# A sparse attention layer: one unit joined on VectorE, part of the last batch weighed by GpSimd, and a written place for every operation

## The chip, the cores and the metric

The kernel runs on one core of one Trainium2 chip. A core has engines with queues of their own that run side by side and meet at semaphores: TensorE (PE in the profile, with its weight loads as PEld), VectorE (DVE), ScalarE (ACT), GpSimd (POOL) and SyncE (SP), which only issues DMA here. The metric is the device time of one execution in microseconds (us); smaller is better.

## The reference, cut to what matters

```python
# x: (16, 1024, 512), adj: (1024, 1024) of 0 and 1, with the diagonal set; W: (512, 512); H, HD = 8, 64
h = jnp.maximum(_layernorm(x, axis=-1), 0.0)
q, k, v = ((h @ W + b).reshape(16, 1024, H, HD) for W, b in ((Wq, bq), (Wk, bk), (Wv, bv)))
scores = jnp.einsum('bihd,bjhd->bhij', q, k) / jnp.sqrt(64.0)
scores = scores + jnp.where(adj == 0, -1e9, 0.0)
weights = jax.nn.softmax(scores, axis=-1)
return x + jnp.einsum('bhij,bjhd->bihd', weights, v).reshape(16, 1024, 512)
```

The adjacency is sparse and very uneven: a few rows have many neighbours, most have a handful. All data are 32-bit floats.

## The kernel before, in words

The kernel never forms the full score matrix. It ranks the 1024 nodes by degree once, cuts the ranked order into eight tiles of 128 rows (tile 0 has the longest rows, tile 7 the shortest), and gives each tile a fixed number of neighbour slots (`CAPS`: 11, 8, 6, 5, 4, 3, 3, 2). What is left of long rows of tile 0 is cut into pieces of four neighbours; the pieces of all rows fill one more group, called tile -1, whose results are added to their owners' rows with a matmul by an owner matrix (`owner_t`).

Slots are handled in *units* of two to four slots (`PARTS`, `UNITS`): fourteen units a batch, four of them for tile 0: (0,0), (-1,0), (0,4) and (0,8), where a pair is the tile and the first slot. In the program's numbering they are units 10 to 13.

For each of the 16 batches, and with two batches in flight at a time:

- `load_x` (GpSimd, an indirect load by the ranked order), `stats`, `variance`, `power`, `shift` and `norm` make the normalized rows; `flip` transposes them on TensorE and `unflip` copies them to SBUF (ScalarE).
- `proj_kv` makes keys and values on TensorE, `evict_kv` copies them out of PSUM, and `store_kv` writes them to a table in DRAM. All eight tiles of a batch must be stored before its first gather.
- `queries` projects the queries of a tile (TensorE). For the pieces, `copy_q` and a matmul by `owner` spread tile 0's queries to the pieces.
- `gather` (GpSimd, an indirect DMA of 512 KB for each slot; the row itself comes by a plain DMA from SP) brings key and value rows of the neighbours into one of six buffers `g`.
- `multiply` and `score` (VectorE) make the scores of a unit, `exponent` (ScalarE) the weights, `row_sums` (VectorE) their sums.
- The values are weighed slot by slot: `weigh_v` on VectorE, `weigh_s` on ScalarE, with eight activations, one for each head, for a slot.
- `fold` adds the slots of a unit to one (VectorE, some on GpSimd). In batches 0 to 14 tiles 1 to 7 are then summed over their units by `join` on VectorE; tile 0's four units are summed by `add_up` on TensorE, in PSUM. In the last batch nothing but tile 7 is folded, and every slot of the other tiles is added by `add_up`.
- `scale` divides by the row sum, `residual` adds x, and `put_out` scatters the 128 rows to the output by an indirect DMA of GpSimd.

The order of all this is not left to a compiler: `planned` lists every operation with its engine, what it follows and which buffers it uses, and in the kernel before a planner (`Plan.ordered`) runs that list against assumed lengths (`LENGTHS`) and priorities (`AT`, `FINE`), and so fixes the order of each engine's queue. The engines then run their queues in order, each waiting at semaphores where data or a buffer isn't ready. Buffers are counted in `POOLS`: 16 for x, 6 for g, 3 for kvt, 2 each for the PSUM tiles of keys and values, queries and sums, 1 for the scaled result `o`.

Where a unit of tile 0 is summed, in `add_up`:

```python
count = 1 if folds(b, B, t, count) else count
for s in range(count):
    nc.tensor.matmul(ACC[b, home], owner_t if t < 0 else ident, v[:, s, :], ...)
```

In the profile L1103 is `multiply`, L1107 `score`, L1111 `exponent`, L1123 `weigh_v`, L1129 `weigh_s`, L1134 `fold`, L1141 `join`, L1157 `add_up`, L1070 the matmul that spreads queries to the pieces, L843 and L841 the projections and their bias, L1093 the gathers, L1207 the sum with x and L1210 `put_out`.

Of the kernel before, what the change touches and what calls it, by code (L numbers as in the profile page):

```python
# [25 lines left out]
F32 = mybir.dt.float32  # L26
# [6 lines left out]
P = 128  # L33
H = 8
# [26 lines left out]
LAST_TILES = (0, 1, 2, 3, 4, 5, 6, 7)  # L61
LAST_ORDER = tuple(UNITS.index(unit) for t in LAST_TILES for unit in PARTS[t])
LAST_DIRECT = (7,)
POOL_FOLDS = ((5, 0), (4, 0), (1, 0), (1, 4), (-1, 0))
# [6 lines left out]
BY_VECTOR_LAST = {2: 1, 3: 1, 4: 1}  # L71
VECTOR_RESIDUAL = (4,)
AT = dict(
    load_x=170.09, stats=-5.83, variance=-6.1, power=-47.58, shift=-11.83, norm=-65.99, flip=-3.5, unflip=-69.44, proj_kv=-0.17,
    evict_kv=-1.04, queries=-0.21, own=7.45, gather=-8.51, score=1.54, exponent=37.66, row_sums=-33.29, share=-103.18,
    weigh_v=-4.42, weigh_s=56.4, fold=-4.42, join=-3.58, add_up=-5.47, direct_residual=3.86, direct_out=-0, more=-116.77,
    pass_on=-0.94, sums=-5.02, scale=-1.48, residual=-38.62, put_out=-47.81, seen=11.6, zero=-5.59, zero_rate=0.56,
    ahead=-14.69, early=0.02, early2=0.33, early3=0.24, first=-60.83, first_rate=7.61, v_late=9.54, key_row=-221.51,
    rank_row=-80.11, rank_d=-9.75, rank_a=45.47, ranks=-75.78, ends=-96.51, list_of=76.9, tell=-79.58, spread=-44.68,
    others=-101.81, spots=-59.47, long_rows=-152.98, long_0=-64.75, long=-72.37, longest=20.9, count=-6.64, pieces=2.43,  # L80
    setup=-64.27, parts=-10.1, spread_bias=-5.47, copy_q=131.7, fetch_q=-35.12, evict_v=0.78, bias_v=-48.9,
)
FINE = {
    ('owners',): -1.5, ('rank_of', 0): 5.46, (-1, 'evict_kv', 7, 0): 0.78, (-1, 'proj_kv', 2, 1): 6.9,
    (-1, 'proj_kv', 6, 0): 9.56, (-1, 'proj_kv', 7, 0): 8.02, (0, 'multiply', 4): 10.01, (0, 'queries', 0, 1): -1.48,
    (0, 'queries', 0, 7): 5, (0, 'weigh_s', 5, 0): -10.62, (1, 'evict_kv', 3, 1): -0.64, (1, 'flip', 1): 0.71,
    (1, 'fold', 11, 1, 1): 0.79, (1, 'fold', 12, 2, 2): 2.15, (1, 'fold', 8, 1, 1): 1.26, (1, 'fold', 8, 2, 2): 2.12,
    (1, 'gather', 8, 3): 0.98, (1, 'join', 9): 3.14, (1, 'multiply', 5): 1.61, (1, 'multiply', 6): 1.34,
    (1, 'proj_kv', 0, 0): -0.95, (1, 'proj_kv', 2, 0): 1.26, (1, 'put_out', 0, 4): -1.57, (1, 'put_out', 0, 5): -2.25,
    (1, 'score', 13): -5.29, (1, 'score', 5): 3.73, (1, 'score', 9): -0.38, (1, 'shift', 1): 3.92, (1, 'weigh_s', 6, 1): 1.85,  # L90
    (1, 'weigh_v', 11): -2.61, (1, 'weigh_v', 9): -1.9, (2, 'add_up', 1): 3.15, (2, 'add_up', 3): 6.42,
    (2, 'evict_kv', 5, 1): 3.83, (2, 'gather', 12, 0): 1.34, (2, 'gather', 3, 1): -1.6, (2, 'gather', 4, 2): -1.63,
    (2, 'gather', 6, 2): -2.75, (2, 'gather', 7, 2): -2.05, (2, 'gather', 8, 3): -1.07, (2, 'gather', 9, 0): 2.03,
    (2, 'gather', 9, 1): 2.13, (2, 'proj_kv', 1, 1): 1.06, (2, 'proj_kv', 2, 1): 1.64, (2, 'proj_kv', 3, 0): 14.3,
    (2, 'proj_kv', 4, 1): -0.54, (2, 'proj_kv', 6, 0): -1.82, (2, 'residual', 0, 4): 2.64, (2, 'residual', 0, 6): 7.2,
    (2, 'score', 7): -2.13, (2, 'store_kv', 6): -3.35, (2, 'variance', 1): 1.8,
# [3 lines left out]
JOIN = False  # L100
BIAS_V = {0: 'DVE', 2: 'DVE', 4: 'DVE', 6: 'DVE'}
PAIRED = ()
FETCH = False


LENGTHS = dict(
    zeros=(0.15, 2.0, 0.0), load_w=(0.2, 2.5, 3.0), load_b=(0.6, 2.2, 0.0), load_adj=(0.2, 2.5, 1.5),
    spread_bias=(0.22, 0.2, 0), copy_bias=(0.47, 0.15, 0), bias_v=(1.43, 0.0, 0),
    setup=(1.0, 0.1, 0), add_bias=(0.22, 0.2, 0), join_acc=(0.602, 0.13, 0),
    parts_at=(0.4, 0.13, 0), warm=(1.3, 0.1, 0), round=(0.58, 0.15, 0), remain=(1.2, 0.1, 0), degree=(1.4, 0.13, 0), no_diagonal=(0.3, 0.1, 0),  # L110
    keys=(0.45, 0.13, 0), flip_row=(0.45, 0.2, 0), copy_row=(0.68, 0.13, 0), rank_of=(1.28, 0.13, 0), ranks=(1.1, 0.13, 0),
    ends=(1.1, 0.13, 0), list_of=(2.46, 0.13, 0), tell=(1.28, 2.5, 0), spread=(1.5, 2.5, 0), collect=(0.05, 2.6, 0),
    others=(1.25, 0.13, 0), perm_of=(0.4, 0.13, 0), spots=(4.0, 0.13, 0), long_rows=(1.25, 4.0, 1.5), long_blocks=(3.4, 0.13, 0),
    longest=(1.02, 0.13, 0), count_pieces=(0.8, 0.13, 0), first_piece=(0.45, 0.2, 0), owners=(0.95, 0.13, 0), flip_owners=(0.27, 0.2, 0),
    copy_owners=(0.25, 0.13, 0), list_pieces=(0.4, 0.2, 0), pieces=(1.0, 0.13, 0), slots=(1.6, 0.13, 0),
    load_x=(1.25, 3.0, 0.68), stats=(0.818, 0.13, 0), variance=(0.1, 0.13, 0), power=(1.2, 0.0, 0), shift=(0.08, 0.13, 0),
    norm=(0.719, 0.13, 0), flip=(0.437, 0.2, 0), unflip=(0.465, 0.15, 0), proj_kv=(3.649, 0.2, 0), evict_kv=(0.465, 0.15, 0),
    store_kv=(0.1, 2.6, 1.36), proj_q=(3.649, 0.2, 0), evict_q=(0.465, 0.15, 0), store_q=(0.1, 2.6, 0.68), fetch_q=(1.25, 3.0, 0.68),
    queries=(3.649, 0.2, 0), copy_q=(0.487, 0.15, 0), gather=(1.25, 3.0, 1.36), multiply=(0, 0.13, 0), score=(0, 0.13, 0),
    exponent=(0.125, 0.14, 0), row_sums=(0.371, 0.13, 0), share=(0.117, 0.13, 0), weigh_v=(0, 0.13, 0), weigh_s=(1.91, 0.14, 0),  # L120
    fold=(0, 0.13, 0), join=(0.602, 0.13, 0), add_up=(0.858, 0.2, 0), more=(0.133, 0.13, 0), pass_on=(0.14, 0.2, 0),
    scale=(0.602, 0.13, 0), residual=(0.602, 0.13, 0), put_out=(1.30, 3.0, 0.68), seen=(0.25, 0.13, 0),
)
LENGTHS["fold", "POOL"] = LENGTHS["residual", "POOL"] = (1.43, 0.0, 0)
LENGTHS["evict_kv", "DVE"] = (0.602, 0.13, 0)
LENGTHS["gather", "SP"] = (0.1, 3.0, 1.36)
LENGTHS["load_x", "SP"] = (0.2, 2.5, 0.75)
LENGTHS["store_kv", "POOL"] = (1.25, 2.6, 1.36)
PAIR = {1: 0.602, 2: 1.131, 3: 1.668, 4: 2.198}
SHARED = ("fold", "join", "bias_v",  "weigh_v", "residual", "scale", "power")  # L130


BY_UNIT = ("gather", "multiply", "score", "exponent", "weigh_v", "weigh_s", "fold", "join", "add_up", "share")
BY_TILE = ("load_x", "stats", "norm", "flip", "unflip", "proj_kv", "evict_kv", "store_kv", "bias_v")
BY_HOME = ("queries", "row_sums", "residual", "put_out", "scale", "more", "pass_on", "copy_q", "store_q", "fetch_q", "seen")


def spot_of(key, B):

    name, *rest = key
# [6 lines left out]
    elif name in BY_HOME:  # L149
        b, at = rest[0], 0  # L150
    else:
        return (name, *rest)
    return (min(b, 1) + (b == B - 1), name, at, *rest[1:])


class Plan:

# [1244 lines left out]
```

## Time and profile before

| | |
|---|---|
| three runs | 1630.22, 1632.87, 1635.69 us; median 1632.87 |
| the profiled execution | 1644.55 us, span 1642.9 us, mean granted clock 0.989 |
| busy: TensorE, VectorE, ScalarE, GpSimd | 96%, 93%, 88%, 76% of the span |
| DMA | 531.71 MB, 324 GB/s over the span |
| weighing on ScalarE (L1129) | 4696 activations of 337 ns, 1154.4 us |
| additions on TensorE (L1157) | 208 matmul passes of about 0.6 us each as recorded |
| joins on VectorE (L1141) | 45 of 672 ns |

A busy share is an average over the start, fourteen or so periods that look alike, and an end in which the last batch is alone. The start and the end are therefore read by themselves, from stretches of time and from the instructions in order. A matmul of 32-bit floats shows as two records, and their ends overlap: what one costs is read from one start to the next. The profiled execution took 11.7 us longer than the median of the three runs; sums are made against its own time.

### The profile page before, as it was taken

The numbers are of one execution on the slowest core, as the hardware profiler recorded it, in microseconds if no ns is written. First come the engines' busy times: TensorE is split into PE (matmuls) and PEld (weight loads), VectorE is DVE, ScalarE is ACT, GpSimd is POOL, SyncE is SP. The second block draws the span as 40 slices with busy tenths as digits, with TensorE's granted clock in tenths as the row PEclk, the third lists the DMA queues.
The fourth block names the chain that finished last, engine by engine and source line by source line (L and its number), as shares of the span: only waits on it lengthen the run. The fifth ranks groups of instructions, "written<-read, shape, count | busy, mean of one in ns | idle before, by whom it ended". The sixth has DMA issues, their size and how long they took to land. (4 is left out here: it accounts for less than half of the span.)

```text
span 1642.9 us, 19494 instructions
## 1 busy us (share of the span) xinstructions
PE 1574.6 (96%) x4236; PEld 729.9 (44%) x4236; DVE 1525.6 (93%) x2081; ACT 1444.9 (88%) x5420; POOL 1248.7 (76%) x1184
## 2 busy tenths in 40 slices
PE   6899999999999999999999999999999999999696
PEld 3454444444444444444444444444444444444232
DVE  7779999999999999999999999999999999999996
ACT  4258989998998989899898999989999998999885
POOL 3766878778878877887878877888787778777764
PEclk9999999999999999999999999999999999999898
DMA  6487989989899998989999998999989899998993
GB/s 246 138 313 242 360 328 338 362 318 365 313 347 329 355 355 318 358 318 349 336 331 365 327 370 302 337 337 348 352 322 349 301 346 336 348 354 312 339 359 123
DMA packets 150740, 531.71 MB, mean 324 GB/s; under 512 B 19916, under 2 KB 19916, under 8 KB 150616
## 3 DMA queue, kind: packets, MB, share of 16 engines
q0 software_dynamic: 109840, 390.70, 66.6%
q1 hardware_dynamic: 40776, 139.71, 22.0%
q14 instruction: 89, 0.73, 0.1%
q8 instruction: 35, 0.57, 0.1%
HBM read 429.51 MB, written 100.82 MB: 323 GB/s over the span
## 5 line engine op out<-in xcount | busy, mean ns | idle before, releaser
L1129 ACT ACTIVATE g<-g,weights 128x64 f32<-128x64 f32 x4696 | 1154.4, 337 | 18.8 <-DVE weights L1116 10.8
L1093 POOL DMA_INDIRECT g<-kv,index x608 | 638.9, 1051 | 221.7 <-issue 176.4
L843 PE MATMUL pq<-wq,hT 128*128 128x512 f32 x1024 | 460.3, 592 | 0.0
L843 PE MATMUL pk<-wk,hT 128*128 128x512 f32 x960 | 432.9, 594 | 0.0
L843 PE MATMUL pv<-wv,hT 128*128 128x512 f32 x960 | 431.5, 592 | 0.1
L1107 DVE TENSOR_REDUCE weights<-g 128x32 f32<-128x2048 f32 (+2 forms) x224 | 422.5, 1888 | 0.7
L1103 DVE TENSOR_TENSOR g<-g,pq 128x1536 f32<-128x1536 f32 (+2 forms) x208 | 388.7, 1870 | 27.5 <-DMA g<-kv,index 11.3
L843 PEld LDWEIGHTS pq<-wq,hT 128*128 128x128 f32 x1024 | 194.6, 190 | 221.5 <-issue 217.8
L843 PEld LDWEIGHTS pk<-wk,hT 128*128 128x128 f32 x960 | 182.9, 191 | 216.9 <-issue 212.9
L843 PEld LDWEIGHTS pv<-wv,hT 128*128 128x128 f32 x960 | 180.1, 190 | 191.6 <-issue 187.6
L1134 DVE TENSOR_TENSOR g<-g 128x512 f32<-128x512 f32 (+1 forms) x301 | 253.5, 844 | 8.1 <-ACT g L1129 5.3
L1210 POOL DMA_INDIRECT out_dram<-x,perm x128 | 137.8, 1076 | 40.8 <-issue 18.9
L788 POOL DMA_INDIRECT x<-in_x_dram,perm x128 | 131.7, 1029 | 38.5 <-issue 37.6
L1134 POOL TENSOR_TENSOR g<-g 128x512 f32<-128x512 f32 x90 | 114.0, 1275 | 5.0 <-DVE g L1134 2.8
L1111 ACT ACTIVATE weights<-weights 128x32 f32<-128x32 f32 (+2 forms) x224 | 49.8, 223 | 77.2 <-DVE weights L1107 60.5
L1123 DVE TENSOR_TENSOR g<-g,weights 128x512 f32<-128x512 f32 x149 | 109.0, 739 | 2.9 <-ACT weights L1111 2.8
L1207 POOL TENSOR_TENSOR x<-x,o 128x512 f32<-128x512 f32 x67 | 86.1, 1285 | 17.8 <-DVE o L1198 14.9
L823 ACT ACTIVATE h<-x,shift,rstd 128x512 f32<-128x512 f32 x120 | 92.4, 806 | 0.5 <-DVE shift L813 0.5
L830 PEld LDWEIGHTS pht<-ident,h 128*128 128x128 f32 x512 | 64.3, 145 | 63.6 <-issue 54.2
L1157 PE MATMUL acc<-g,ident 128*128 128x512 f32 x170 | 83.9, 607 | 2.4 <-ACT g L1129 1.5
L835 ACT COPY hT<-pht 128x512 f32<-128x512 f32 x128 | 73.0, 575 | 14.9 <-PE pht L830 13.1
L797 DVE BATCH_NORM_STATS2 st<-x 128x6 f32<-128x512 f32 x120 | 81.5, 679 | 2.5 <-DMA x<-in_x_dram,perm 2.4
(242 smaller groups left out, 1108.3 us busy)
## 6 DMA issues: line engine op xcount, KB each, us to landing
g<-kv SPq DMA_DIRECT2D x128, 512.0 KB
kv<-kvt SPq DMA_DIRECT2D x120, 512.0 KB
g<-kv,index POOLq DMA_INDIRECT x608
adj<-in_adj_dram SPq DMA_DIRECT2D x8, 512.0 KB
x_first<-in_x_dram SPq DMA_DIRECT2D x8, 256.0 KB
x<-in_x_dram,perm POOLq DMA_INDIRECT x128
out_dram<-x,perm POOLq DMA_INDIRECT x128
wk<-in_L_gnn_Wk_dram SPq DMA_DIRECT2D x1, 1024.0 KB
```

The lines of the kernel that those rows point to most:

```text
L788: nc.gpsimd.indirect_dma_start(out=X[n][:], out_offset=None, in_=x_rows, in_offset=on(ap=perm[:, t : t + 1], axis=0), element_offset=b * N * D
L823: nc.scalar.activation(HN[n], X[n], AF.Relu, bias=shift, scale=scale)
L843: nc.tensor.matmul(pt, HT[n][:, c, :], W[name][:, c, :], start=(apart and c == 0), stop=(n != -NT and c == DC - 1))
L1093: nc.gpsimd.indirect_dma_start(out=G[i][:, s].rearrange("p j d -> p (j d)"), out_offset=None, in_=KV[b % len(KV)][:], in_offset=on(ap=inde ...
L1103: nc.vector.tensor_tensor(k, k, Q[b, t][:, None, :].to_broadcast([P, count, D]), ALU.mult)
L1107: nc.vector.tensor_reduce(weights[:, w, :], heads(G[i][:, :count, 0, :]), AX.X, ALU.add)
L1123: nc.vector.tensor_tensor(v, v, own.to_broadcast([P, n, H, HD]), ALU.mult)
L1129: nc.scalar.activation(v[:, h, :], v[:, h, :], AF.Identity, scale=weights[:, c + s, h : h + 1])
L1134: engine.tensor_tensor(v[:, 0:n], v[:, 0:n], v[:, first : first + n], ALU.add)
L1157: nc.tensor.matmul(ACC[b, home], owner_t if t < 0 else ident, v[:, s, :], start=(u == added_up(b, B, home)[0] and s == 0), stop=(u == adde ...
L1207: (nc.vector if residual_by_vector(b, B, t) else nc.gpsimd).tensor_tensor(rows, rows, add, ALU.add)
L1210: nc.gpsimd.indirect_dma_start(out=out_rows, out_offset=on(ap=perm[:, t : t + 1], axis=0), in_=X.pop(b * NT + TILES.index(t))[:], in_offse ...
```

## The change

Four things are changed together.

1. In batches 0 to 14 the fourth unit of tile 0, (0,8), is no longer added by TensorE. VectorE joins it to the third, (0,4), and TensorE adds the two at once (`PAIRED`).
2. In the last batch nine slots are weighed by GpSimd (`weigh_p`), one in each of nine units, where ScalarE did it. VectorE weighs one slot of each unit, as before.
3. In the last batch VectorE, not GpSimd, adds x for tiles 4, 5, 6 and 7. The scaled results of the last batch lie in the two buffers of `h`, not in the one of `o`; units 7 and 9 of that batch, and with them others, change turns (`LAST_ORDER`).
4. The planner and its lengths go. Each operation has a number of its own (`PLACES`): one set for what is done once, one for the first keys and values, one each for batches 0, 1, 2, one for batches 3 to 13, one for batch 14 and one for batch 15. Each engine's queue is sorted by these numbers. This moves instructions on every engine. At the start, TensorE has three matmuls of its own right after the first transposes (`warm_pe`), and SP loads more x tiles and three adjacency blocks ahead of Wk. At the end, the last five scatters of batch 14 stand among and behind the gathers of batch 15, those of tiles 1 and 0 behind the last of them.

A copy that the piece lists did not need is dropped in two places, and so is code that no path used.

```diff
-LAST_TILES = (0, 1, 2, 3, 4, 5, 6, 7)
-LAST_ORDER = tuple(UNITS.index(unit) for t in LAST_TILES for unit in PARTS[t])
+LAST_ORDER = (10, 11, 12, 13, 8, 6, 9, 7, 4, 3, 5, 2, 1, 0)
+LAST_BY_POOL = {(0, 0): 1, (-1, 0): 1, (0, 4): 1, (1, 0): 1, (1, 4): 1, (2, 0): 1, (2, 3): 1, (3, 0): 1, (4, 0): 1}
-BY_VECTOR_LAST = {2: 1, 3: 1, 4: 1}
+LAST_BY_VECTOR = {}
+LAST_VECTOR_RESIDUAL = (5, 4, 6, 7)
-AT = dict(
...
+PERIOD = 95.290021
+PLACES = {
+    'once': dict(
...
+        load_w=(-11.05, 8.59, 8.7,),
+        load_b=(-37.43, -22.46, -37.77,),
+        load_adj=(-32.34, -7.47, 2.51, -4.27, 2.04, 2.09, -32.29, -34.65,),
+        warm_pe=(-43.81,),
...
+    'next': dict(
...
+        put_out=(119.83, 147.92, 153.92, 195.74, 222.34, 239.09, 289.32, 388.72,),
...
+    'last': dict(
...
+        put_out=(326.77, 344.67, 296.49, 296.56, 295.05, 263.96, 296.53, 291.63,),
+        weigh_p=(208.43, 161.86, 144.12, 147.11, 134.86, 147.08, 104.82, 104.91, 123.45,),
...
-PAIRED = ()
+PAIRED = (13,)
...
+    def places(self):
+        count = {}
+        result = []
+        for key, *_ in self.ops:
+            b, spot = spot_of(key)
+            kind = kind_of(b, self.batches)
+            at = count[b, spot[0]] = count.get((b, spot[0]), -1) + 1
+            result.append(PLACES[kind][spot[0]][at] + PERIOD * (b or 0))
+        return result
...
+        pool = by_pool(b, B, u)
+        if pool:
+            weighed.append(("weigh_p", k))
+            add(("weigh_p", k), "POOL", [weights], [g])
+        for s in range(count - vector - pool):
...
-            o = ("o", b, home)
+            o = ("o", b, home) if b < B - 1 else ("h", "o", home)
...
 def residual_by_vector(b, B, t):
-    return t in VECTOR_RESIDUAL and (b < B - 1 or t in LAST_DIRECT)
+    return t in (VECTOR_RESIDUAL if b < B - 1 else LAST_VECTOR_RESIDUAL)
...
+        def warm_pe():
+            p = ps_a.tile([P, D], F32, tag="acc", name="p_warm")
+            for _ in range(3):
+                nc.tensor.matmul(p, ident, scratch[:, 2, :D], start=True, stop=True)
...
+        def weigh_p(i):
+            b, t, w, c, count = unit(i)
+            to = count - by_vector(b, B, i % NU)
+            n = by_pool(b, B, i % NU)
+            v = heads(G[i][:, to - n : to, 1, :])
+            own = weights[:, c + to - n : c + to, :, None]
+            nc.gpsimd.tensor_tensor(v, v, own.to_broadcast([P, n, H, HD]), ALU.mult)
```

`pairs_up`, `join` and `added_up` were there before, without a unit to act on: with (13,) in `PAIRED` the join adds the folded unit 13 onto the buffer of unit 12, and the addition of unit 12 follows it.

## The prediction

> **What bounds the kernel now.** I read the page's busy times first, then the answer by stretches of time, and last the instructions in order of time at both ends, where the stretches differ.
>
> The page's first part, by engine:
>
> ```profile
> PE 1574.6 (96%) x4236; PEld 729.9 (44%) x4236; DVE 1525.6 (93%) x2081; ACT 1444.9 (88%) x5420; POOL 1248.7 (76%) x1184
> ```
>
> TensorE leads, with VectorE close behind. The stretches tell where. Their columns are the length, then busy time and instruction count of PE, PEld, DVE, ACT, POOL, then granted clock, DMA share and GB/s:
>
> ```profile
> 75.00:80.00 5.00, 2.23 (x6) 0.69 (x4) 0.99 (x9) 0.00 (x0) 2.84 (x3) 1.00 0.74 219
> 800.00:900.00 100.00, 99.61 (x271) 46.33 (x270) 96.86 (x120) 92.73 (x354) 80.97 (x74) 1.00 0.93 338
> 1540.00:1550.00 10.00, 0.19 (x1) 0.19 (x2) 8.97 (x11) 10.00 (x44) 7.99 (x9) 0.72 0.94 335
> 1580.00:1590.00 10.00, 8.34 (x20) 3.35 (x19) 9.19 (x7) 9.77 (x41) 5.06 (x6) 1.00 0.97 353
> 1620.00:1625.00 5.00, 5.00 (x13) 2.28 (x12) 4.48 (x8) 4.29 (x19) 0.35 (x1) 1.00 0.01 2
> ```
>
> From 200 to 1500 us TensorE is 98 to 100% busy: it sets the period. The matmul that expands the queries for the pieces comes every 95.76 us (276.1 to 1042.2 us for eight batches). VectorE follows at about 95%, DMA at 93%. Around 77 us TensorE stands still (6.23 us, ended by ScalarE's h), and after 1540 us ScalarE, VectorE and DMA carry the time. In TensorE's order of time an addition into tile 0's sum occupies 0.86 us, from its start to the next instruction's:
>
> ```profile
> 976.30 1.02 PE L1157 MATMUL acc<-g,ident 128*128 128x512 f32 x2
> 977.16 0.60 PE L830 MATMUL pht<-ident,h 128*128 128x128 f32 x4
> ```
>
> The end, in GpSimd's order of time (start, length, instruction, idle time before it):
>
> ```profile
> 1609.08 0.94 POOL L1093 DMA_INDIRECT g<-kv,index  x1 [0.30 <-issue]
> ...
> 1612.29 1.01 POOL L1210 DMA_INDIRECT out_dram<-x,perm  x1 [0.28 <-POOL x L1207]
> ...
> 1630.12 0.98 POOL L1210 DMA_INDIRECT out_dram<-x,perm  x1 [1.02 <-issue]
> ...
> 1633.89 0.98 POOL L1210 DMA_INDIRECT out_dram<-x,perm  x1 [0.28 <-POOL x L1207]
> 1637.63 0.96 POOL L1210 DMA_INDIRECT out_dram<-x,perm  x1 [2.76 <-DMA out_dram<-x,perm]
> ```
>
> The last gather is issued at 1609.08; 33.8 us later all is over. The last scatter waits 2.76 us for the landing of the one before: scatters to the output go one at a time, 3.74 us apart when nothing else holds them.
>
> **What the Trainium skill says.** "DMA: Bandwidth & Descriptors", section "Two DMAs through the same engine are not ordered": the only order an author has is the completion semaphore, on which the issuing engine waits. The scatters do this, 3.74 us each. Its section "Anatomy of one DMA — SWDGE (gpsimd) path" gives 2.0 us and bytes by 436 GB/s, so an estimated 2.6 us for 256 KB; the chain of waits has 2.28 to 3.22 us from issue to landing, and detection and issue come on top. "SBUF — State Buffer", "Who interferes with whom": a VectorE instruction with two SBUF inputs and a GpSimd instruction that reads SBUF exclude each other. The trace agrees: VectorE's fold at 1628.08 took 1.58 us beside a GpSimd sum, 0.68 us elsewhere. "TensorE: Matmul & The Clock Gate", "What's actually happening": an idle array runs at half clock until about 3.4 us of activity. The first key projection took 4.83 us, the next 3.60.
>
> **The change, part by part.**
>
> *Fourth unit joined (batches 0 to 14).* TensorE loses one addition of 0.86 us per batch, 14 of them before the last projection: 14 x 0.86 = 12.0 us. VectorE gains a join like those of L1141, 0.67 us, and goes from 91.3 busy of 95.76 to 92.0 of 94.9, or 97%. ScalarE's work is the same. If TensorE stays the bound all 12.0 us are gained; if VectorE's thin slack (4.5 us a batch before, 2.9 after) lets waits through, less, and in the worst case all is lost. The wait that is added: TensorE's addition of the third unit now waits for the join, and all projections queue behind it. In the old trace queries of tile 7 start at 968.1 and VectorE's multiply of tile 7 at 973.25. In the new order VectorE then does that multiply, a half fold, the score, three short folds, sums and the join, 1.2+1.2+1.2+0.6+0.6+0.6+0.4+0.6 and a small shift: 6.5 us, so the join ends 11.6 us after the queries' start. TensorE reaches the addition after three query projections and one addition, 3 x 3.65 + 0.86 = 11.8 us. That is a margin of 0.2 us, so I count 0.7 us of gain per batch: -9.8 us, ends -12.0 and 0.
>
> *Start.* SP's queue now puts Wk behind six x tiles and three adjacency blocks, 3.1 MB instead of 0.5. At the 344 to 388 GB/s of the first 12 us Wk lands some 7 us later, about 15 us. The first projection, at 12.99 before, starts near 17, but on a warmed clock (3.6, not 4.83): TensorE is 2.5 us late at 20 us. Against this, VectorE counts adjacency from about 9 us instead of 12.0, and only four of GpSimd's list scatters stand ahead of the first permuted x load where seven stood; the first such load, at 63.8 us, should go near 53. TensorE's stall at 77 us (6.23 us, then about 1.8 us of cold clock) came from ScalarE stuck on an eviction that waited 9.05 us with the next norms behind it; the new order has those norms ahead. Stall gone: 2.5 - 6.2 - 1.8 - 2.1 (two small waits that a later start covers) = -7.7. Stall kept: +2.5. I take -4.
>
> *The last batch.* Count from the end of its last projection, A = 1534 before. Before: first gather A+5, last A+75, end A+109. ScalarE loses nine slots of eight activations, 9 x 1.94 = 17.5 us, and with them the waits for buffers that GpSimd's gathers had there (the longest 4.75 us). GpSimd gets nine weighings, priced by its 128x512 fold at 1.28 us plus 0.15 to issue. From first gather to last it now issues 38 gathers (1.25 each, 47.5), eight weighings (11.4), three scatters of batch 14 (3.9), two sums (2.9), one fold (1.4): 67 us, so with no waits the last gather goes at A+71, 4 us better. Walking the queues I find each buffer and exponent ready before GpSimd asks. VectorE's four sums with x cost 4 x 0.68 = 2.7 us; it has about 85 us of work after A and ends near A+92, before the scatters do. The lock can add at most 9 x 1.28 = 11.5 us to VectorE, still under that cover.
>
> What is new is where scatters stand: two of batch 14 (tiles 1 and 0) are moved behind the last gather. After it come a scatter, two sums and a weighing, and then nine scatters in a row: batch 15's tile 2 near A+78, then eight more at 3.74 us, 29.9 us, and 5.3 us from the last issue to the end as now: A+113, that is +4 us. Once this chain stands, compute that ends sooner no longer matters. Ends: -6 (scatters spaced 2.6 us, the skill's estimate) and +10 (spaced 4.7 us, as between 1612.29 and 1617.01).
>
> The fixed orders in the middle (places instead of a planner) issue the same instructions but for the join; I cost them at nothing, covered by the pools' slack on ScalarE and VectorE. Dropped copies in the piece lists (two of about 0.2 us) lie under TensorE's projections.
>
> Sum: -9.8 - 4 + 4.2 = -9.6 us. Against the profiled execution that is 1644.55 to about 1635 us; the shown runs have a median 11.7 us lower, so 1632.87 - 9.6 = 1623 us.
>
> **The rivals.**
> A. *Everything pays.* Join in full (-12), stall gone (-7.7), scatters closely spaced or overlapping (-6): 1607 us. For: TensorE has no idle time to lose in the middle. Against: the 2.76 us wait on a landed scatter.
> B. *VectorE or DMA become the period.* At 97% and 94% the gain of the join goes into waits; start -4 and tail +4 cancel: 1633 us. For: VectorE already waits 11 us in all for gathers. Against: it had 4.5 us per batch to spare.
> C. *Slower: TensorE waits for the join.* If ScalarE's last weighings come late, the join ends late by L and every projection of that batch with it. Fourteen batches pay 14 x L against 12.0: with start and tail even it decides at L = 0.86 us. At L = 2 us the net is +16: 1649 us.
> The change may also not do what it says in one respect: sums on VectorE speed nothing if the scatters behind them are a chain; that is in my forecast.
>
> **How the numbers follow.** Forecast (1616 to 1628) 0.46; A (1605 to 1615) 0.20; B (1628 to 1638) 0.18; C (over 1638) 0.16. 0.3% is 4.9 us, about what a measurement of this kernel can tell from no change. Faster 0.66, same 0.18, slower 0.16. The range leaves out the far half of A and of C: 1608 to 1640.
>
> **What would show it.** Right: a period near 95.0 us in the middle, one addition fewer for tile 0 in each batch, TensorE still 99% busy; no 6 us stall before 85 us; the last gather 71 us after the last projection and then nine scatters about 3.7 us apart with GpSimd waiting on the output's landings, all compute over 15 us before the end. Wrong: waits of TensorE's addition for the join in every batch (C), an unchanged period with VectorE above 97% (B), or an end within 30 us of the last gather (A).

## The result: 1.3% slower

The changed kernel takes 1651.78 us against 1632.71 us before (medians of four runs each): ratio 1.0129, 95% interval 1.0085 to 1.0173. Two later series gave 1.0109 (1.0068 to 1.0150) and 1.0103 (1.0075 to 1.0131). By these ratios it is slower by 17 to 21 us; the forecast was 10 us faster, and 1652 us lies above the range.

From one series of runs to the next the median of the kernel before itself moved between 1633 and 1658 us. So every ratio below is to the kernel before in the same series, and a difference in us is that ratio times its median. Profiles are compared within a series, except for the two shown here and where it is said.

The profile after, read like the one before. First the page's busy times:

```profile
PE 1570.6 (95%) x4212; PEld 723.4 (44%) x4212; DVE 1533.9 (93%) x2098; ACT 1428.5 (87%) x5348; POOL 1275.4 (77%) x1189
```

TensorE has 4.0 us less than before, and VectorE 8.3 us more. This sum also grows where matmuls follow a gap or run on a slow clock, so the count by stage below goes by the distance between starts instead. The stretches of time (length, then busy time and count of PE, PEld, DVE, ACT, POOL, then clock, DMA share, GB/s):

```profile
75.00:80.00 5.00, 5.00 (x17) 2.52 (x16) 4.29 (x28) 3.45 (x6) 3.78 (x5) 1.00 0.76 227
800.00:900.00 100.00, 97.86 (x263) 44.99 (x262) 95.13 (x126) 93.09 (x353) 81.70 (x75) 1.00 0.95 336
1540.00:1550.00 10.00, 2.72 (x5) 1.60 (x6) 8.79 (x11) 10.00 (x44) 8.31 (x8) 0.63 0.95 312
1580.00:1590.00 10.00, 10.00 (x27) 4.41 (x26) 9.25 (x12) 8.39 (x37) 7.36 (x9) 1.00 0.91 305
1620.00:1625.00 5.00, 5.00 (x13) 2.26 (x12) 4.45 (x9) 3.54 (x16) 2.46 (x3) 1.00 0.28 105
```

The stall at 75 to 80 us is not in this profile, as forecast (whether that is the change's doing, see below). In the middle TensorE is 97.9% busy where it was 99.6%, and VectorE is at 95.1%, below the 96.9% of before: the engine that got work is not the one that filled up. TensorE's order of time shows what it waits for now:

```profile
198.44 2.08 PE L1364 MATMUL acc<-g,owner_t 128*128 128x512 f32 x2 [2.73 <-POOL g L1345]
...
684.81 1.12 PE L1364 MATMUL acc<-g,owner_t 128*128 128x512 f32 x2 [1.76 <-POOL g L1345]
...
974.17 1.12 PE L1364 MATMUL acc<-g,owner_t 128*128 128x512 f32 x2 [0.41 <-POOL g L1345]
975.13 0.38 PE L1057 MATMUL pq<-bias_parts,chosen 128*128 128x512 bf16 x1
```

The addition of the pieces' unit waits for GpSimd's last fold of it, in most batches (14.1 us in 11 waits). The addition that the prediction feared for, that of the third unit, comes 8.9 us later and waits as well, for the join. The profile names no releaser there ("issue"), but the orders of time of VectorE and TensorE show one:

```profile
499.34 0.64 DVE L1352 TENSOR_TENSOR g<-g,g 128x512 f32<-128x512 f32 x1
...
500.08 1.10 PE L1364 MATMUL acc<-g,ident 128*128 128x512 f32 x2 [0.46 <-issue]
```

L1352 is the join, which writes what this addition reads, and the addition starts 0.10 us after the join's end. That is so in all six of these waits before 1530 us (2.7 us), in all nine of e6 (4.3 us), and e2, the changed kernel without the join, has none of them.

The end, in GpSimd's order of time:

```profile
1607.94 0.96 POOL L1296 DMA_INDIRECT g<-kv,index  x1
1609.21 1.39 POOL L1412 DMA_INDIRECT out_dram<-x,perm  x1 [0.30 <-issue]
...
1616.23 1.03 POOL L1412 DMA_INDIRECT out_dram<-x,perm  x1 [0.77 <-POOL x L1409]
1619.27 0.96 POOL L1412 DMA_INDIRECT out_dram<-x,perm  x1 [2.01 <-DMA out_dram<-x,perm]
...
1640.50 0.96 POOL L1412 DMA_INDIRECT out_dram<-x,perm  x1 [2.90 <-DMA out_dram<-x,perm]
1643.97 0.96 POOL L1412 DMA_INDIRECT out_dram<-x,perm  x1 [2.51 <-DMA out_dram<-x,perm]
```

Ten scatters follow the last gather; from 1616.23 us on they come 3.0 to 4.0 us apart. For five of these eight distances the profile names the landing of the scatter before as what ended the wait.

### Where the time went, by stage

A stage is cut at TensorE's expansion of the pieces' queries of a batch (L1070 before, L1283 after) and at A, the start of the last matmul of the last projection of keys or values (1533.4 us before, 1535.2 after). Within a stage I add up TensorE's *lost time*: what the distance between the starts of two successive matmuls has over the matmul's length at full clock (0.429 us for one of 128x512 in f32), so idle time and slow clock together. TensorE's work from its first projection to A is 1481.1 us before and 1469.1 us after: the 12.0 us of fourteen additions less.

The predicted change of a stage is what the prediction had to expect of its lost time: 0.7 us of 0.86 us gained leaves 0.16 us a batch.

| stage | first pair | second pair (e5, e6) | predicted change |
|---|---|---|---|
| TensorE's first projection starts | 13.0 -> 17.4 | 13.1 -> 16.8 | late by 4 |
| lost from there to batch 0's expansion | 16.2 -> 3.3 | 9.0 -> 3.0 | with the line above: -4 |
| lost in batches 0 to 2 | 5.5 -> 13.7 | 6.5 -> 13.0 | under +1 |
| lost in batches 3 to 11 | 15.5 -> 26.0 | 11.2 -> 22.9 | +1.4 |
| lost from batch 12 to A | 2.1 -> 5.8 | 3.0 -> 5.8 | under +1 |
| from A to the end | 109.4 -> 114.4 | 107.8 -> 115.5 | +4.2 |

The start is better, by 8.5 and 2.3 us. Everything behind it is worse: batches 0 to 2 by 8.2 and 6.5, batches 3 to 11 by 10.5 and 11.7, the end by 5.0 and 7.7. In batches 3 to 11 that is more than the work that TensorE is spared: these nine take 868.9 us where they took 866.5, and 865.7 where they took 862.2. The first profile of before (1644.55 us) lies 12 us above its median, which is why the first pair shows only 6.7 us of span in all and the second 14.4.

### The profile page after: what moved, and what is told of

It is laid out like the page before. It is cut to its first block, busy times and chain, and to the rows that moved or that the text cites. A ratio compares the mean times of both kernels' runs of the same rounds, so it can differ in the third digit from the quotient of the medians.

```text
span 1649.6 us, 19403 instructions
## 1 busy us (share of the span) xinstructions
PE 1570.6 (95%) x4212; PEld 723.4 (44%) x4212; DVE 1533.9 (93%) x2098; ACT 1428.5 (87%) x5348; POOL 1275.4 (77%) x1189
## 5 line engine op out<-in xcount | busy, mean ns | idle before, releaser
L1340 ACT ACTIVATE g<-g,weights 128x64 f32<-128x64 f32 x4624 | 1139.3, 337 | 27.7 <-DVE weights L1319 23.1
L1004 POOL DMA_INDIRECT x<-in_x_dram,perm x128 | 143.2, 1119 | 37.9 <-issue 34.2
L1345 POOL TENSOR_TENSOR g<-g 128x512 f32<-128x512 f32 x90 | 116.6, 1296 | 13.1 <-DVE g L1345 11.4
L1039 ACT ACTIVATE h<-x,shift,rstd 128x512 f32<-128x512 f32 x120 | 93.9, 810 | 29.6 <-DVE shift L1029 25.3
L1409 POOL TENSOR_TENSOR x<-x,o 128x512 f32<-128x512 f32 x64 | 82.3, 1285 | 10.5 <-DVE o L1400 9.4
L1364 PE MATMUL acc<-g,ident 128*128 128x512 f32 x140 | 69.8, 620 | 15.3 <-issue 10.5
L1046 PE MATMUL pht<-ident,h 128*128 128x128 f32 x512 | 75.1, 274 | 7.1 <-ACT h L1039 5.8
```

The lines of the kernel that those rows point to most:

```text
L1004: nc.gpsimd.indirect_dma_start(out=X[n][:], out_offset=None, in_=x_rows, in_offset=on(ap=perm[:, t : t + 1], axis=0), element_offset=b * N * D
L1039: nc.scalar.activation(HN[n], X[n], AF.Relu, bias=shift, scale=scale)
L1046: nc.tensor.transpose(PH[n][:, c, :], hn[:, ts(c, P)], ident)
L1340: nc.scalar.activation(v[:, h, :], v[:, h, :], AF.Identity, scale=weights[:, c + s, h : h + 1])
L1345: engine.tensor_tensor(v[:, 0:n], v[:, 0:n], v[:, first : first + n], ALU.add)
L1409: (nc.vector if residual_by_vector(b, B, t) else nc.gpsimd).tensor_tensor(rows, rows, add, ALU.add)
```

## The experiments

Three theories run through them. O: the join pays, and the fixed order of the middle lets TensorE wait, above all for GpSimd's fold. J: the join itself costs what it saves or more. V: it does not help to relieve TensorE, since VectorE or the transfers set the period. A fourth, S, is on the end alone: the row of scatters sets it.

### The join alone, and the changed kernel without it

In e1 the kernel before keeps its own order and gets only the join. In e2 the changed kernel keeps its order and loses it.

```diff
 e1, on the order of before, in batches 0 to 14 (k is the fourth unit):
-  TensorE: add_up(k-1) ... add_up(k)
+  TensorE:                 add_up(k-1)          (where add_up(k) stood)
+  VectorE: join(k) straight after fold(k,1,1), ahead of a share of the next batch
 e2, on the changed order:
-  VectorE: join(k)
+  TensorE: add_up(k) straight after add_up(k-1)
```

> The kernel before, its own order of instructions, with one thing changed: in batches 0 to 14 VectorE joins the fourth unit of tile 0 to the third straight after the fourth's last fold, and TensorE's one remaining addition stands where the fourth's stood. Theory O (the fixed order of the middle lets TensorE wait; the join itself is sound): TensorE's work falls by 12.0 us before the last projection and most of it is gained, 1620 to 1625 us against 1632.7. Theory J (the join itself costs, by VectorE's 0.67 us or by TensorE's wait for it): no gain or slower, 1633 to 1650 us. Theory V (VectorE or DMA set the period whatever is done to TensorE): unchanged, 1631 to 1635 us.

> The changed kernel, its own order, with the join taken out: TensorE adds the fourth unit straight after the third, as an addition of its own, and VectorE does not join. Theory O: TensorE gets 12.0 us of work back in an order in which it already waits; where those waits are for engines that run on, part of it is absorbed: 1655 to 1664 us against 1651.8. Theory J: the loss of the middle was the join's, so without it 1635 to 1645 us. Theory V: unchanged within 3 us, 1649 to 1655 us.

e1: ratio to before 1.0005 (0.9988 to 1.0022), that is +0.8 us (-2.0 to +3.6): the join is worth nothing. e2: 1.0129 (1.0099 to 1.0160) in the same series, where the changed kernel did not run; in its other series it had 1.0129, 1.0109 and 1.0103. So taking the join out gives nothing back either. Theory J's stronger form (the join is the loss) falls with e2, theory O's "the join itself is sound" falls with e1. What is left is that the join's gain and its cost cancel, and the next runs part the two.

### TensorE's addition left out, VectorE's addition added, a VectorE fold left out

```diff
 e7, order of before:   -  TensorE: the fourth unit's add_up   (its rows are missing from the sum)
 e8, order of before:   +  VectorE: fold(k,1,1) done twice      (one 128x512 addition more)
 e17, order of before:  -  VectorE: fold(k,1,1)                 (one slot missing from the sum)
 e18:                   both e7's and e17's
```

> The kernel before with the fourth unit's addition for tile 0 left out in batches 0 to 14 (its rows are missing from the sum) and nothing put in its place: TensorE has 12.0 us less to do before the last projection, VectorE nothing more. If TensorE is the bound and the join's cost on VectorE ate its gain (theory J): 10 to 12 us faster than before. If TensorE's work does not set the period (theory V): within 4 us of before, as the join alone was.

> The kernel before with one VectorE addition of 128x512 more in batches 0 to 14, straight after the fourth unit's last fold (it repeats that fold's addition, so the sum is not the reference's), and TensorE's additions as they were: VectorE has 0.67 us a batch more, 10 us in all. If VectorE sets the period (theory V): 7 to 12 us slower than before. If TensorE is the bound and VectorE has slack (the prediction): within 3 us of before.

> The kernel before with the last fold of tile 0's fourth unit left out in batches 0 to 14 (one of its slots is missing from the sum): VectorE has one 128x512 addition of 0.67 us less a batch, TensorE all its additions. If VectorE counts in full (theory V): 8 to 13 us faster than before. If TensorE alone is the bound at the old length: within 3 us of before.

> The kernel before with both left out in batches 0 to 14: the last fold of the fourth unit on VectorE and the fourth unit's addition on TensorE (the unit is missing from the sum). If both count and add up (theory V, one loop through the engines): 18 to 25 us faster than before. If the two gains are one and the same slack: 10 to 13 us, no more than the addition left out alone.

| run | TensorE | VectorE | ratio to before | us |
|---|---|---|---|---|
| e7 | 0.86 us less a batch | as before | 0.9928 (0.9900 to 0.9957) | -11.8 |
| e8 | as before | 0.67 us more a batch | 1.0080 (1.0051 to 1.0110) | +13.1 |
| e17 | as before | 0.67 us less a batch | 0.9992 (0.9980 to 1.0004) | -1.3 |
| e18 | 0.86 us less | 0.67 us less | 0.9938 (0.9916 to 0.9961) | -10.1 |
| e1 | 0.86 us less | 0.67 us more | 1.0005 (0.9988 to 1.0022) | +0.8 |

TensorE's addition was worth its full 12 us: it was the bound, as the prediction said. (In e7 TensorE also no longer waits for VectorE's last fold of the fourth unit, but in e5, the kernel before in that series, no addition waits for it between 180 and 1530 us.) VectorE had no room for 0.67 us more at this place, though it was busy only 93% of the span; the prediction, for which e8 stays within 3 us, missed. e1 and e7 say the same once more: their profiles have the same order of instructions on every engine, but for the fifteen joins of e1, and +0.8 against -11.8 us makes 12.6 us for these. But VectorE is not a second bound of equal rank: a fold less at the same place gains nothing (e17), and adds nothing to what TensorE gains (e18). Theory V, "VectorE counts in full", missed with both of its last forecasts.

How 0.67 us on an engine with idle time gets through to TensorE is seen in what ScalarE waits for between 180 and 1530 us (total, times, longest). In e5, the kernel before in the series of e7 and e8:

```profile
ACT weights L1111 <- DVE weights L1107: 75.2, 61, 2.8
ACT g L1129 <- DVE weights L1116: 11.7, 32, 0.9
```

With one VectorE addition more (e8):

```profile
ACT weights L1111 <- DVE weights L1107: 72.0, 55, 2.5
ACT g L1129 <- DVE weights L1116: 26.7, 31, 2.2
```

L1116 is the share of a unit's weights, which VectorE makes and ScalarE's weighing (L1129) needs; the share of the next batch's first unit stands closely behind the place where the addition went in, with a row sum, a reciprocal and a fold between. ScalarE already waited there, and it now waits 15.0 us more. ScalarE also copies the queries of tile 0 for TensorE's expansion, and that comes later: TensorE's waits for the copy go from 11 (11.1 us) to 13 (19.8 us). TensorE, about 99% busy, can't make up a wait. It also waits for the doubled fold itself, 2.4 us in 5 waits. In the run with the fold left out (another series) the first of these waits is short:

```profile
ACT g L1129 <- DVE weights L1116: 3.0, 15, 0.4
```

TensorE's waits for the copy fall to 7 (4.2 us) there, but the time stays: with all its additions to do TensorE is the bound, and with 0.67 us more on VectorE the other chain is. Why a chain that leaves room for 0.86 us less on TensorE has none for 0.67 us more on VectorE is not settled. That the path through share and copy carries e8's whole 13.1 us is a reading of these waits, and was not tried apart either. Against it speaks that the faster e7 has 18.0 us of waits for the copy as well. The changed kernel has its join ahead of a share too, and in e6 ScalarE waits 22.7 us for shares. But in other series that wait is 13.5 us in e2, without the join, and 13.5 and 13.3 us in e4 and e13, with it: in the changed order it does not tell the join's cost.

### The join on GpSimd

```diff
 e12, order of before, batches 1 to 13:
-  TensorE: add_up(k-1) ... add_up(k)
+  GpSimd:  join(k) among the next batch's gathers;   TensorE: add_up(k-1) where add_up(k) stood
```

> The kernel before with the join of the fourth unit to the third done by GpSimd in batches 1 to 13 (by VectorE in 0 and 14), TensorE's fourth addition removed. If VectorE's 0.67 us a batch is what ate the gain of 12 us (as the kernel with the addition left out, -11.8 us, and the kernel with one VectorE addition more, +13.1 us, say), GpSimd with its quarter of idle time can take it: 6 to 12 us faster than before. If the join costs wherever it stands (TensorE's wait for it, or gathers that go 1.3 us later): within 4 us of before, or slower.

Ratio 1.0102 (1.0058 to 1.0145), +16.9 us: worse than on VectorE. Batches 3 to 11 took 884.1 us, against 873.2 us in e9 and 872.2 in e10, which have before's order there and no join. TensorE waits for the join itself now, between 300 and 1450 us:

```profile
PE acc L1166 <- POOL g L1150: 21.7, 12, 2.5
```

That is rival C of the prediction, with GpSimd in VectorE's stead. GpSimd was busy about three quarters of the time, but among its gathers the 1.28 us of the join end too late for TensorE's addition.

### The wait of TensorE for GpSimd's fold

In e3 this fold goes ahead of the next batch's gathers in batches 0 to 13, in e14 only in batches 3 to 13.

```diff
 GpSimd, at the turn of a batch:
+  fold(11,1,1)
   gather(0,1) gather(1,2) put_out(tile 1) gather(1,1)
-  fold(11,1,1)
   gather(2,2)
```

> The changed kernel with one operation moved on GpSimd in batches 0 to 13: the last fold of the pieces' unit goes ahead of the next batch's first gathers and of the scatter of tile 1, where it stood behind two or three of them. Theory O: TensorE's 11 waits for this fold (14.1 us in the profile) vanish and most of that comes off: 1638 to 1644 us against 1651.8. Theory V: the waits move to other instructions, 1648 to 1653 us. Theory J: unchanged, or a new wait of TensorE for the join of the fourth unit, about as long, takes its place, 1648 to 1655 us.

> The changed kernel with the last fold of the pieces' unit ahead of the next batch's gathers on GpSimd, in batches 3 to 13 only (moved in batches 0 to 2 as well, it had taken 6.5 us there and given 7 later). Theory O (TensorE's wait for this fold, 1.0 to 1.8 us a batch, sets the period of the middle): 5 to 9 us faster than the changed kernel, a period nearer 95.6 than 96.4. Theory V (all engines share one loop, a wait removed comes back elsewhere): within 3 us of the changed kernel.

> The changed kernel, unchanged, on the same chip as the two variants of its middle beside it: 1.1 to 1.3% slower than before.

e3: 1.0103 (1.0076 to 1.0131) beside e2's 1.0129. e14: 1.0079 (1.0059 to 1.0099) beside 1.0103 (1.0075 to 1.0131) for the changed kernel in the same series (e13): 4 us of 1662, with intervals that overlap; in the profiles batches 3 to 11 take 871.3 us with the fold moved and 870.4 without. In this pair the 9 us of waiting are not there to be had. In e13, TensorE from 465 to 1330 us:

```profile
PE acc L1364 <- POOL g L1345: 9.0, 8, 1.6
PE pht L1046 <- ACT h L1039: 3.9, 6, 1.2
PE acc L1364 <- issue: 3.7, 8, 0.5
```

In e14 the wait for the fold is gone, and in its place GpSimd waits for VectorE's half of the fold, ahead of all its gathers, and TensorE's additions wait longer where the profile names no releaser:

```profile
POOL g L1348 <- DVE g L1348: 12.4, 11, 1.3
...
PE acc L1367 <- issue: 9.7, 9, 1.4
PE pht L1049 <- ACT h L1042: 4.1, 6, 1.0
```

What these additions wait for is again the join: all nine start 0.10 us after its end (L1355 here). So the wait for the fold was removed and the wait for the join grew from 3.7 to 9.7 us in its place, as theory J had expected of e3. Theory O falls in this form in the pair e13 and e14. It is not quite dead: in the series of e3, which moved the fold too, batches 3 to 11 took 864.9 us, against 871.4 in e2 and 872.1 in e4, and e3 lost as much in batches 0 to 2.

### The order of the middle

e9 has the changed kernel's start, and the order of before from batch 0 on, with before's join-free sums and last batch. e11 has the changed start, join and last batch, with the order of before from batch 0 into batch 14. e15 is like e11, but with batch 0 as changed, a blend of both orders in batches 1 and 2, and the order of before from batch 3.

```diff
 a list of operations in place of the places:
-  order = planned(B).ordered()
+  order = changed order of the start, then for each engine the order that the kernel before has, then the changed last batch
```

> The changed kernel's start (loads, sorting, lists, projections of the shared keys and values) in its order; from batch 0 on the order of the kernel before, with TensorE's fourth addition, the old last batch and the planner's order in the middle. Against before on the same chip. If the gain of the start, 6 to 12 us at the first expansion of the pieces' queries in the two pairs of profiles, lasts to the end: 5 to 12 us faster. If the middle takes it back because something else was late anyway: within 3 us of before.

> The changed kernel with its start, its join and its last batch, but the middle (batches 0 to 13 and most of 14) in the order of the kernel before, with the join straight after the fourth unit's last fold as in the join alone. It differs from the changed kernel in nothing but the order of the middle. Against before on the same chip: theory O (the changed order of the middle costs 8 to 12 us of its own): start -8, join 0, tail +6, so 0 to 6 us faster than before, where the changed kernel is 18 us slower. If the order of the middle costs nothing, 15 to 20 us slower, like the changed kernel.

> The changed kernel's start, batch 0, join and last batch, with the order of before (and the join) from batch 3 to batch 13 and a blend of both orders in batches 1 and 2. Theory O: its batches 3 to 11 lose no more time than before's, and with the lead of the start it ends 6 to 14 us ahead of the changed kernel, at 0.3 to 0.8% over before. If the order of the middle is not the cause: within 3 us of the changed kernel.

e9: 1.0028 (1.0010 to 1.0047), +4.6 us. e11: 1.0091 (1.0060 to 1.0121), +15.1 us. e15: 1.0209 (1.0183 to 1.0234), +34.4 us. None of the three is what it was meant to be: each has a long stall near the seam. In e9 TensorE stands still where the two orders meet:

```profile
92.86 1.97 PE L1614 MATMUL pht<-ident,h 128*128 128x128 f32 x8 [14.11 <-ACT h L1607]
```

In e11 it is 12.44 us at 90.79, and in e15 batches 0 to 2 have periods of 102.8, 102.2 and 105.0 us. How much of it the seam makes is open: e16, whose start has the order of before, stands still for 10.36 us at the same place. So e9 doesn't tell what the changed start is worth, and neither e11 nor e15 whether batches 0 to 2 would have been faster in the order of before. What can be used is a stage away from the seams. Batches 3 to 11, in two series:

| run | order there | join | time | TensorE's lost time |
|---|---|---|---|---|
| e13 | changed | yes | 870.4 | 27.5 |
| e15 | before | yes | 871.1 | 31.5 |
| e16 | before | no | 865.2 | 14.2 |
| e4 (other series) | changed | yes | 872.1 | 29.2 |
| e2 | changed | no | 871.4 | 20.7 |
| e1 | before | yes | 865.8 | 22.3 |

In the first series the two orders take the same time with the join, and without it the nine batches take 5 us less. In the second the changed order takes 6 us more than the order of before, and the join makes no difference in it. Each is a single profile, e15's behind its long stalls. So whether the changed order of these batches costs anything of its own stays open. Batches 0 to 2 are another matter: 301.5 us in e13 against 290.0 in e16, TensorE's lost time 16.5 against 6.3. These batches have places of their own in the changed kernel. The profiles of the changed order lose 11.9 to 16.5 us there (e3 with its moved fold 21.1). Those with the order of before lose 5.5 to 9.2, but for 12.1 (e12, with its join), 13.2 (e10) and 13.6 (e11), so a single profile doesn't decide it; the three pairs, 5.5 -> 13.7, 6.5 -> 13.0 and 6.3 -> 16.5, agree. That it is the order and not the join is seen in e1 and e2: 289.0 us for these three batches in the order of before with the join, 299.4 in the changed order without it. It is most plainly seen on GpSimd. The first gather of batch 1 goes 6.6 us earlier in e6 than in e5, that of batch 2 1.1 us later. The waits in between are many and short, in TensorE, VectorE, ScalarE and GpSimd alike (the longest: TensorE 2.69 us for GpSimd's fold, ScalarE 3.60 us for the shift of a norm). Which of them is the cause stays open.

### The last batch

e10 is the kernel before up to batch 14 (with the three warming matmuls and without the dropped copies) with the changed last batch. e16 is e10 with the nine slots given back to ScalarE. e4 is the changed kernel with two scatters of batch 14 moved up.

```diff
 e16:  -  GpSimd: weigh_p(k)      +  ScalarE: weigh_s(k, last slot) behind the unit's others   (nine units)
 e4, GpSimd in the last batch:
+  put_out(14, tile 1)  ahead of weigh_p(9);   put_out(14, tile 0)  behind residual(14, 0)
   ... the last five gathers ...
-  put_out(14, tile 1), put_out(14, tile 0)
```

> The kernel before up to batch 13, with the changed kernel's last batch: GpSimd weighs nine slots, four of its sums with x are on VectorE, and the units, gathers and scatters stand in the changed order from the seam in batch 14 on. Against before on the same chip. The prediction counts +4 us for this (chain of scatters behind the last gather); the two pairs of profiles give +5 and +8 us from the last projection to the end: 3 to 9 us slower. If the loss of the tail is inherited from the middle: within 2 us of before.

> The kernel with the changed last batch alone (0.76% slower than before), with the nine slots given back from GpSimd to ScalarE, each straight after the unit's other ScalarE slots; order, scatters and sums as they were. If the weighings on GpSimd cost (they delay its gathers by 11 us of work): faster than the changed last batch alone, at 0 to 0.4% over before. If the scatters behind the last gather set the end: the same 0.5 to 1.0% over before, with ScalarE up to 17 us later but still inside the chain. If ScalarE becomes the bound: over 1.2%.

> The changed kernel with two scatters moved on GpSimd in the last batch: the outputs of tiles 1 and 0 of batch 14 go ahead of the last five gathers instead of behind them, so that eight scatters stand behind the last gather in a row and not ten. Theory S (the end is a chain of scatters about 3.5 us apart): two links of 3.5 us come off the chain, the last gather goes 2.6 us later, the end comes 3 to 6 us sooner, 1646 to 1649 us against 1651.8. Rival (the end is set by VectorE and ScalarE's work after the last gather, which comes 2.6 us later): unchanged or 2 to 3 us slower, 1652 to 1655 us.

From A, in us (VectorE's last is its last work on the output or the sums):

| run | last gather | VectorE's last | last scatter issued | end |
|---|---|---|---|---|
| before, e5 | 73.9 | 95.0 | 102.6 | 107.8 |
| changed, e6 | 74.3 | 98.0 | 109.8 | 115.5 |
| before's last batch, e9 | 78.8 | 99.9 | 107.1 | 112.4 |
| changed last batch, e10 | 79.0 | 101.0 | 114.0 | 119.2 |
| weighed by ScalarE, e16 | 80.4 | 102.7 | 116.1 | 121.4 |
| two scatters earlier, e4 | 77.1 | 98.9 | 108.8 | 114.5 |

e10: 1.0076 (1.0051 to 1.0101), +12.6 us. Its profile shows 6.9 us of that behind A, against e9 in the same series; the rest is not located (its single profile also loses 13.2 us in batches 0 to 2, which have the order of before). In both pairs VectorE ends within 3 us of its old time, while the last scatter goes 7 us later: ten scatters instead of six stand behind the last gather, one by one. e16: 1.0086 (1.0056 to 1.0116): with the weighings on ScalarE the end is no sooner, so their move to GpSimd is not what costs. (The two are from different series.)

e4: 1.0079 (1.0053 to 1.0105) in the series of e2 (1.0129) and e3 (1.0103). Its end stands at A + 114.5, theirs at A + 114.9 and A + 115.4. The forecast of 3 to 6 us missed in the profile. Its ratio is 0.50 and 0.24% under theirs, with intervals that overlap, so the times don't decide it. With two scatters fewer the row begins at A + 84.1, when the first sum of the last batch is ready, and its seven distances of 3.0 to 4.5 us end no sooner than the nine did: two links had lain in time that waited for that sum anyway.

### The pair in one series

> The kernel before, unchanged, for a profile from the same chip as the three runs beside it. Theory O (order of the middle) and theory V (VectorE or DMA sets the period) both expect its TensorE to lose about as much time to gaps from the first projection to the last as in the profile shown, 39 us of 1520; if the chip alone changes that by over 10 us, profiles of different chips can't be compared stage by stage.

> The changed kernel, unchanged, on the same chip. Theory O: 1.3% slower than before again, 17 to 23 us, with TensorE's waits for the last fold of the pieces' unit near 14 us. If the loss of the middle is the chip's and not the order's, under 10 us.

e5's TensorE lost 29.6 us from its first projection to A, where the first profile of before lost 39.4; e6 lost 44.6. The ratio is 1.0109 here, and TensorE's waits for the fold are 9.9 us in 10 waits between 180 and 1530 us.

## Why the prediction was wrong

*The join: the step that failed.* "If TensorE stays the bound all 12.0 us are gained", and "a margin of 0.2 us, so I count 0.7 us of gain per batch: -9.8". Measured +0.8 us (e1), the worst end that the prediction gave this term. The first half was right: TensorE's addition is worth 11.8 us (e7). What failed is the price of the join, which was set at nothing because a "thin slack" of 2.9 us a batch would be left to VectorE, and because the only wait that I followed was TensorE's own for the join. The added 0.67 us a batch costs 13.1 us (e8), or 12.6 (e1 against e7). The sentence "ScalarE's work is the same" was true and beside the point: ScalarE's *waits* grew in e8, for the shares that VectorE makes behind the addition; that they are the path of the cost is argued, not shown. The waits of the kernel before showed ScalarE waiting for VectorE at exactly that line (13 times between 480 and 1430 us, 4.7 us). This is rival B (the period stays, 1633 us) for this part of the change; its sign, "VectorE above 97%", was not: VectorE is at 95%. Rival C's wait is there in the changed order, though not in e1: 0.45 us a time behind the wait for the fold, and 0.6 to 1.4 us in e14, where the fold is out of the way. C needed 0.86 us a batch to cancel the gain. So the margin of 0.2 us, too, was wrong by about 1.3 us there (9.7 us in nine waits).

With no gain from the join and all else as forecast the sum would have been 1633 us, inside the range. What carried the kernel above it stands in other terms.

*The middle's fixed orders, "at nothing".* This term failed too. For batches 3 to 11 it is open (870.4 against 871.1 us in one series, 872.1 against 865.8 in another). It was wrong for batches 0 to 2, which have tables of their own: TensorE loses 6.5 to 10.2 us more there, 4 to 8 after the 2.6 us of additions that it is spared. I had looked at a batch from the middle and taken it for all of them.

*The start, -4 us.* Size about right: 2.3 us better in the second pair, 8.5 in the first, and the first projection comes 4 us late, as said. But the mechanism is not shown, and the hit is in part luck: the stall goes with the series, not with the order. The kernel before has none in e5, and e1, which has the same start, waits 6.11 us; the changed kernel has none in e6, and a wait of 5.20 us near 89 us in e13. At the end of batch 2 the second pair has lost the gain, and the first keeps 2.6 us of it. (The four terms for "stall gone" add up to -7.6, not -7.7.)

*The last batch, +4.2 us.* Mechanism right, size under, in the profiles by a little: last gather at A + 72.7 (forecast A + 71), then nine distances between scatters, of 3.0 to 7.0 us (forecast 3.7), the end at A + 114.4 (forecast A + 113). The cost is 5.0 and 7.7 us from A to the end, and 12.6 us in the times of e10. GpSimd's weighings cost nothing that e16 shows, and gain nothing at the end, as forecast.

*The sum.* Instead of -9.8 - 4 + 4.2: the join +1, the start -2.3 to -8.5, batches 0 to 2 +4 to +8, the end +5 to +8. That makes about +1.5 to +15 us, with the profiled pairs at 6.7 and 14.4; the timed runs say +17 to +21. Several microseconds are not located, among them the 5.7 that e10 has over its profile; the cause of the 2.4 to 3.5 us more in batches 3 to 11 is open too.

Of the signs that were to show it: one addition fewer, the last gather and the row of scatters came as forecast, and so did the absence of a stall before 85 us, in the two profiles of the pairs. The period near 95.0 us did not: it is 96.5 us over batches 3 to 11, where it was 96.3.

## What to carry to other kernels

An engine with idle time need not have room for one more instruction: here 0.67 us a batch on VectorE, about 95% busy in the middle, cost 0.87 us a batch. Before moving work onto such an engine, look up who waits for the next instructions in its order (here the share, 11.7 us of ScalarE's waits in e5), not only its busy share. Where a second chain is nearly as long as the bound, work taken from the bound and put on that chain may be worth nothing. Where one engine waits twice in a row, taking away the first wait may only lengthen the second: moving the fold gave the time to the join (e14). And a wait that the profile doesn't name can be named by looking for what ended just before it in the other engines' order. Where first batches have an order of their own, cost them apart from the middle.

A later place for the join in the order of before, behind the share and the next multiplication, follows from this, and was not tried; in the changed order TensorE waits for the join as it is.

## What the runs showed of the hardware

Two things were not expected. After a wait of 2.73 us TensorE's matmuls ran at about half their speed in one profile: the addition at 198.44 us took 2.08 us instead of 1.02 to 1.12. In the second profile of the changed kernel nearly the same wait, 2.69 us, cost nothing (1.12 us). The Trainium skill, "TensorE: Matmul & The Clock Gate", section "What's actually happening", tells of the half clock after an idle window of about 3.4 us; these profiles show that a shorter gap may or may not bring it. The same wait (2.69 to 2.73 us) was followed by slow matmuls in e2, e4, e13 and e14 as well. And scatters to the output in a row were 3.0 to 4.0 us apart, some closer than the 3.74 us of the profile before, none as close as the estimate of 2.6 us that the prediction had made from "DMA: Bandwidth & Descriptors", "Anatomy of one DMA — SWDGE (gpsimd) path".
